# Column marks of a sparse four-layer graph network: summed by halves on GpSimd instead of a maximum on VectorE

## The chip, the cores and the metric

The kernel runs on one core of a Trainium2 chip. The metric is the device time of one execution in microseconds (us): before the change the median of three runs is 1175.17 us (1168.04 to 1184.51). The profiled execution has a span of 1172.0 us from its first to its last instruction. The engines of the core are called as the profile calls them: PE (TensorE matmul), PEld (its weight load), DVE (VectorE), ACT (ScalarE), POOL (GpSimd), SP (SyncE, which here only issues transfers).

## What is computed

Four layers of a graph network run over x (4096 rows of 128 features) and an adjacency matrix adj (4096 x 4096). Each layer is x = x + layer(relu(layernorm(x)), adj). Layers 0 and 1 multiply adj with the features (once and twice), layer 2 is an attention over the marked pairs, and layer 3 sums GELU messages over them:

```python
neigh = adj @ x                                               # layer 0
T_next = 2.0 * (L_tilde @ T_curr) - T_prev                    # layer 1, after T_curr = L_tilde @ x
Tau = adj_matrix.T * jnp.exp(jnp.maximum(0.2 * C, C))         # layer 2
messages = jax.nn.gelu(s[:, None, :] + d[None, :, :] + msg_b, approximate=False)
aggregated = jnp.einsum('ijd,ij->id', messages, adj)          # layer 3
```

Most of adj is zero. An entry (i, j) off the diagonal is non-zero with a probability that falls with both i and j, so the first rows and columns are dense and the rest is nearly empty. The kernel finds the non-zero entries once, while it runs layer 0, and from then on works with lists.

## The kernel before

The matrix is taken in 32 blocks of 128 rows (NB), in 16 stripes of 256 rows (ROWS) and in 16 stripes of 256 columns (COLS). For each stripe the blocks that are dense enough are read whole ("near"). The other rows or columns that have an entry in the stripe form a list, cut into chunks of 128, and each chunk is fetched by an indirect gather that POOL issues (line 551).

**Finding the entries.** For each block b of 128 rows, two halves of 1 MB are read by `read_adj` (line 766 issues on SP's queue) into three buffers. `mark` (line 776, ACT) turns each half into one byte per element, 0x38 for a non-zero, in one of four mask tiles (128 x 4096 bytes, or 1024 words of four elements). Then `scan` works on DVE, in this order: line 787 clears the diagonal in the block's own 32 words; line 791 takes, for each of the 16 column stripes, the maximum of its 64 words, and writes it to column b of `col_raw` (128 x 16 x 32); line 796 ORs the word's number into the mask (tile `words`, 128 x 1024); line 798 multiplies by "mask is non-empty", so that words without an entry become zero; and line 805 takes the eight largest words of each segment (MAX8), which are the candidates for the entry lists.

**Row lists.** `row_flags` counts the marks of a row stripe with matmuls on PE (line 704), and `pairs` (lines 641 to 681, DVE, with ACT line 630 and PE lines 645, 646 and 664 between) makes the stripe's list, `fetch_row` and `seg_row`. Layer 0 then gathers, on POOL, for each chunk of the list one tile of adjT (`rseg`, eight buffers) and one of features (`g`, fourteen buffers), PE multiplies them (line 1163), and SP stores `rseg` to a table for the later layers (line 730). Where 512 columns of the result are complete, ACT copies them (line 1172), PE multiplies with the weights (line 604), and DVE adds them to x (line 1000) and normalises.

**Column lists.** They need the marks of all 32 blocks: `all_marked` is set after the last block's line 791. `col_flags` (line 717) then compares `col_raw` of one stripe with EMPTY and runs the same `pairs`; `fetch_columns` gathers the adj chunks (`cseg`), which layer 2 reads.

**The order of the work.** Every step is a Python generator that says which engine it wants and for how long. A planner runs these against a model of the engines while the program is written, and the resulting order is fixed on every engine: each executes its instructions strictly in the order in which the planner recorded them. A step that asks for a tile waits for a free slot (`Slots`), and `give_back` returns the slot when a `Count` of its readers has come to zero. Where the planner sees PE idle it adds filler matmuls (line 617) that keep its clock up. POOL's order holds constants, 12 additions of a bias to x (lines 987 and 1008), and 724 gathers: per layer those for layer 0 (`rseg`, `g` from h_tab), the column chunks (`cseg`), layer 1 (`g` from h_tab and u_tab), the values of single entries (`e_val`), layer 2 (`g` from a_tab) and layer 3 (`m`, `tau` and `e` from d_tab).

Of the kernel before, what the change touches and what calls it, by code (L numbers as in the profile page):

```python
# [12 lines left out]
F32 = mybir.dt.float32  # L13
# [5 lines left out]
I32 = mybir.dt.int32  # L19
AF = mybir.ActivationFunctionType  # L20
ALU = mybir.AluOpType
AX = mybir.AxisListType
# [5 lines left out]
P = 128  # L28
NB = N // P
# [10 lines left out]
EMPTY = struct.unpack("<f", b"\x30" * 4)[0]  # L40
WORDS = N // 4
# [76 lines left out]
RS, CS = 256, 256  # L118
# [3 lines left out]
COLS = [Stripe(i, CS, C_EXTRA) for i in range(N // CS)]  # L122
# [235 lines left out]
def on_dve(n):  # L358
    return "DVE", 0.16 + 1.05e-3 * n
# [19 lines left out]
def sparse_stack(tc, x, adj, adjT, diag, w_self, w_neigh, b0, w1, b1, w2, att_src, att_dst,  # L379
# [7 lines left out]
    nc = tc.nc  # L387
    plan = Plan()
    EARLY = 7
    with ExitStack() as ctx:  # L390
# [4 lines left out]
        def tiles(pool, name, n, shape, dtype=F32):  # L395
            return Slots([pool.tile(list(shape), dtype, name=f"{name}{i}", tag=f"{name}{i}") for i in range(n)])

        def kept(name, shape, dtype=F32):
            return keep.tile(list(shape), dtype, name=name, tag=name)
# [114 lines left out]
        col_raw = kept("col_raw", (P, len(COLS), NB))  # L514
# [198 lines left out]
        def col_flags(s):  # L713
            yield all_marked
            lane = yield lanes
            yield on_dve(NB)
            nc.vector.tensor_scalar(lane["f"], col_raw[:, s.index, :], EMPTY, None, op0=ALU.is_gt)
            yield from pairs(s, lane, fetch_col, seg_col, CS, col_list[s.index])

        row_list = [Event() for _ in ROWS]  # L720
        col_list = [Event() for _ in COLS]
        r_done = [Count(s.cap) for s in ROWS]
        c_done = [Count(s.cap) for s in COLS]
        all_marked = Event()

        def store(ready, t, slots, left, dst, done, size):

# [7 lines left out]
        def give_back(left, slots, t):  # L735
            yield left
            plan.release(slots, t, left.time)
# [23 lines left out]
        def read_adj():  # L761
            for b in range(NB):
                for h in range(2):
                    a = yield raws
                    yield SP
                    nc.sync.dma_start(a, adj[b * P:(b + 1) * P, h * HALF:(h + 1) * HALF])
                    raw_of[b, h] = a
                    raw_here[b][h].set(plan.transfer(P * HALF * 4))

        def mark():  # L770
            for b in range(NB):
                mask_of[b] = mask = yield masks
                for h in range(2):
                    yield raw_here[b][h]
                    yield on_act(HALF + 200, "sigmoid")
                    nc.scalar.activation(mask[:, h * HALF:(h + 1) * HALF], raw_of[b, h], AF.Sigmoid, scale=1e38,  # L776
                                         accum_out=marks[:, 2 * b + h:2 * b + h + 1], saturate=False)
                    plan.release(raws, raw_of[b, h])
                marked[b].set(plan.finish)

        def scan():
            for b in range(NB):
                yield marked[b]
                mask = mask_of[b]
                yield on_dve(32)
                own = mask.bitcast(I32)[:, b * P // 4:(b + 1) * P // 4]
                nc.vector.tensor_tensor(own, own, off_diag.bitcast(I32), op=ALU.bitwise_and)
                bare[b].set(plan.finish)
                plan.start(give_back(mask_left[b], masks, mask), 0)
                yield on_dve(WORDS)  # L790
                nc.vector.tensor_reduce(col_raw[:, :, b], mask.bitcast(F32).rearrange("p (s w) -> p s w", w=CS // 4),
                                        axis=AX.X, op=ALU.max)
                if b == NB - 1:
                    all_marked.set(plan.finish)
                yield on_dve(WORDS)
                nc.vector.tensor_tensor(words, mask.bitcast(I32), spread, op=ALU.bitwise_or)
                yield on_dve(WORDS + 250)
                nc.vector.scalar_tensor_tensor(words.bitcast(F32), mask.bitcast(F32), EMPTY, words.bitcast(F32),
                                               op0=ALU.is_gt, op1=ALU.mult)
                mask_left[b].set(plan.finish)  # L800
                for u in UNITS:
                    if u.block == b:
                        yield "DVE", 0.15 * len(u.segments) + (u.cuts[-1] - u.cuts[0]) / 960
                        for k, (lo, hi) in enumerate(u.segments):
                            nc.vector.max(cand_of[u.number][:, 8 * k:8 * k + 8], words.bitcast(F32)[:, lo:hi])
                        picked[u.number].set(plan.finish)

        picked = [Event() for _ in UNITS]
        valued = [Count(u.cap) for u in UNITS]
# [154 lines left out]
        def read_x():  # L964
            for g in range(NC):
                yield SP
                nc.sync.dma_start(xN[:, g * GB:(g + 1) * GB, :], x_rows[:, g * GB:(g + 1) * GB, :])
                x_here[g].set(plan.transfer(P * BANK * 4))
                if g == 1:
                    for tab in (h_tabs[0], h_tabs[1], u_tab):  # L970
                        nc.sync.dma_start(tab[N:N + 1, :], zero[:, :D])
                    nc.sync.dma_start(a_tab[N:N + 1, :], zero)

        def begin(g):
            yield x_here[g]
            yield x_here[g + 1]
            blocks = slice(g * GB, (g + 2) * GB)
            yield from norm(blocks, hA[:, blocks, :])
            for k in range(2):
                h_done[g + k].set(plan.finish)  # L980
            yield SP
            nc.sync.dma_start(rows_in(h_tabs[0])[:, blocks, :], hA[:, blocks, :])
            landed = plan.transfer(2 * P * BANK * 4)
            for k in range(2):
                h0_table.set(landed)
            yield "POOL", 2.5
            nc.gpsimd.tensor_add(xN[:, blocks, :], xN[:, blocks, :], by_block(b0_sb, 2 * GB))
            for k in range(2):
                blocks = slice((g + k) * GB, (g + k + 1) * GB)
                yield from to_features(blocks, hA[:, blocks, :])  # L990
# [492 lines left out]
        def weights():  # L1483

            yield "DVE", 0.5
            nc.vector.tensor_sub(w02, w1_sb[:, 0, :], w1_sb[:, 2, :])
            nc.vector.tensor_scalar_mul(w22, w1_sb[:, 2, :], 2.0)
            p = yield banks
            yield on_pe(P)
            nc.tensor.transpose(p[:, :P], w2_sb[:, :D], ident)  # L1490
            yield on_act(P)
            nc.scalar.copy(w2T, p[:, :P])
            yield on_pe(2)
            nc.tensor.matmul(p[:, P:P + 2], w2T, att_sb, start=True, stop=True)
            yield "DVE", 0.5
            nc.vector.tensor_copy(w2_sb[:, D:], p[:, P:P + 2])
            nc.vector.tensor_copy(dst_w, w2_sb[:, D + 1:D + 2].to_broadcast([P, P]))
            plan.release(banks, p)
# [68 lines left out]
        with tc.tile_pool(name="scan", bufs=1) as scanning:  # L1567
            rsegs = tiles(scanning, "rseg", 2048 // RS, (P, RS))
            masks = tiles(scanning, "mask", 4, (P, N), F8)
            raws = tiles(scanning, "raw", 1, (P, HALF))  # L1570
            raws = Slots([dst[:, :HALF], dst[:, HALF:]] + raws.items)
            words = scanning.tile([P, WORDS], I32, name="words", tag="words")
            plan.filler = fill
            plan.start(read_x(), -9)
            plan.start(read_adj(), -8)
            for g in range(0, NC, 2):
                plan.start(begin(g), g * 1e-2 - 8.5)
            plan.start(mark(), -8.6)
            plan.start(scan(), -4)
            plan.start(weights(), 3)  # L1580
            for s in ROWS:
                if s.cap:
                    plan.start(row_flags(s), -9)
            for part in (loads, gathers, products):
                plan.start(part(), 0)
            for s in COLS:
                if s.cap:
                    plan.start(col_flags(s), s.index * 1e-2 - 1.5)
            plan.start(fetch_columns(), 4)
            plan.run(lambda: layers[0].through.time is not None and all(p.time is not None for p in picked)  # L1590
                     and len(rsegs.free) == len(rsegs.items))
# [5 lines left out]
        for i in range(2):  # L1597
            def lane_tile(name, width, dtype=F32):
                return second.tile([P, width], dtype, name=f"{name}_{i}", tag=f"{name}_{i}")
            lane = {k: lane_tile(k, -(-most // 2) + 2 * GB) for k in ("et", "ev", "epop", "ecum", "evf")}  # L1600
# [3 lines left out]
            n = max(sum(u.cap for u in g.units) for g in GROUPS)  # L1604
# [403 lines left out]
```

## Time and profile before

| What | us |
|---|---|
| median of three runs | 1175.17 |
| profiled execution, span | 1172.0 |
| first gather on POOL (`rseg`) | at 87.24 |
| last of 32 maxima (line 791) begins | at 325.53 |
| first column gather (`cseg`) | at 348.03 |
| last gather's issue ends | at 1141.35 |
| 32 maxima, line 791, busy in all | 39.1 |
| 32 ORs, line 796 | 39.5 |
| 32 products, line 798 | 39.1 |
| POOL busy, share of the span | 771.8, 66% |

The page gives, for each engine, busy time and share, then the span in 40 slices whose digits are tenths of busy time, then the costliest groups of instructions: line, engine, operation, output and inputs, count, busy time, mean duration of one in ns, and the idle time of the engine just before them with what ended it. The timeline lists instructions in order with their start and duration; idle time ahead of one stands in brackets with what released it. Idle time of an engine that is not the bottleneck costs nothing.

### The profile page before, as it was taken

To read this page: it belongs to the slowest core of one execution; us is meant where nothing else is said; L and a number is where in the kernel's file an instruction comes from. 1 tells how busy PE (TensorE), PEld (TensorE's weight loads), DVE (VectorE), ACT (ScalarE), POOL (GpSimd) and SP (SyncE) were. 2 spreads that over 40 slices of the span, in tenths; PEclk is the share of its full clock that TensorE was granted. 3 is DMA by queue.
4 is the path that set the end of the run, shared out by engine and by line. 5 is a ranking of instruction groups with operands and counts; after the bars stand their busy time and mean duration, and the time that the engine had idled before them with its cause. 6 is when DMAs were issued, how large, how long until landed. Compare 5 with 4: busy or idle time off the path is not lost. (4 is left out here: it accounts for less than half of the span.)

```text
span 1172.0 us, 19272 instructions
## 1 busy us (share of the span) xinstructions
PE 965.2 (82%) x5782; PEld 669.7 (57%) x5782; DVE 887.9 (76%) x3443; ACT 577.5 (49%) x1228; POOL 771.8 (66%) x831
## 2 busy tenths in 40 slices
PE   5888887878888888788888879899999976678783
PEld 2555665545555665576676654455555555566562
DVE  5799988877878886576888866665666585577895
ACT  3985556654622212232434457576767652234553
POOL 5127746545437677777777778777777777777770
PEclk9979989888789999998989989898999878889997
DMA  7999999999846978889865653443445222222321
GB/s 221 348 349 394 349 407 359 352 309 334 294 127 174 301 217 275 245 272 315 247 204 175 184 150 97 127 129 102 131 131 154 71 69 67 54 68 68 77 74 33
DMA packets 175417, 236.04 MB, mean 201 GB/s; under 512 B 22452, under 2 KB 155336, under 8 KB 167112
## 3 DMA queue, kind: packets, MB, share of 16 engines
q1 hardware_dynamic: 148904, 186.45, 46.9%
q0 software_dynamic: 26400, 48.27, 16.7%
q8 instruction: 48, 0.79, 0.3%
q14 instruction: 65, 0.53, 0.1%
HBM read 203.41 MB, written 31.23 MB: 200 GB/s over the span
## 5 line engine op out<-in xcount | busy, mean ns | idle before, releaser
L551 POOL DMA_INDIRECT e_val<-in_adj,e_at x158 | 163.0, 1032 | 48.0 <-issue 40.1
L551 POOL DMA_INDIRECT g<-h_tab,fetch_row x136 | 134.6, 990 | 41.1 <-issue 27.9
L551 POOL DMA_INDIRECT rseg<-in_adjT,seg_row x68 | 68.8, 1012 | 90.3 <-issue 42.3
L1146 PE MATMUL acc<-big,hA 128*128 128x256 f32 x448 | 122.0, 415 | 2.0 <-DMA big<-in_adjT 2.0
L617 PEld LDWEIGHTS <-nothing 128*128 128x128 f16 x732 | 74.9, 105 | 82.0 <-issue 20.7
L617 PE MATMUL pick<-nothing 128*128 128x512 f16 x430 | 114.2, 413 | 0.0
L551 POOL DMA_INDIRECT cseg<-in_adj,seg_col x74 | 70.9, 958 | 43.6 <-issue 17.3
L1146 PEld LDWEIGHTS acc<-big,hA 128*128 128x128 f32 x448 | 89.4, 210 | 14.5 <-DMA big<-in_adjT 2.6
L776 ACT ACTIVATE mask<-dst 128x2048 fp8e4<-128x2048 f32 x43 | 81.8, 1904 | 26.8 <-DMA dst<-in_adj 26.7
L551 POOL DMA_INDIRECT m<-d_tab,e_col x79 | 76.8, 972 | 24.1 <-issue 13.4
L551 POOL DMA_INDIRECT g<-a_tab,fetch_col x74 | 75.7, 1023 | 22.5 <-issue 12.5
L1163 PE MATMUL acc<-big,g 128*128 128x256 f32 x272 | 77.4, 417 | 9.7 <-DMA big<-r_tab 6.5
L1243 DVE TENSOR_TENSOR tau<-e,big 128x512 f32<-128x512 f32 (+3 forms) x61 | 54.5, 893 | 38.2 <-ACT e L1239 34.0
L551 POOL DMA_INDIRECT tau<-d_tab,e_col x67 | 66.2, 988 | 21.2 <-issue 11.3
L617 PE MATMUL bank<-nothing 128*128 128x512 f16 x302 | 79.8, 401 | 0.0
L551 POOL DMA_INDIRECT g<-u_tab,fetch_row x68 | 64.5, 949 | 20.7 <-issue 8.8
L577 ACT ACTIVATE junk<-xN,stat 128x128 f32<-128x128 f32 x128 | 51.3, 401 | 49.0 <-DVE stat L573 38.5
L1146 PE MATMUL acc<-big,hB 128*128 128x256 f32 x224 | 60.9, 411 | 11.3 <-DMA big<-in_adjT 11.3
L1163 PE MATMUL acc<-rseg,g 128*128 128x256 f32 x136 | 53.4, 501 | 16.8 <-DMA g<-h_tab,fetch_row 16.7
L898 DVE SCALAR_TENSOR_TENSOR ehit<-ehit,pos,pick 128x32 f32<-128x32 f32 (+7 forms) x158 | 38.7, 285 | 36.2 <-ACT ehit L895 35.9
L1163 PEld LDWEIGHTS acc<-big,g 128*128 128x128 f32 x272 | 52.6, 207 | 21.4 <-issue 7.5
L895 ACT COPY ehit<-pick 128x192 f32<-128x192 f32 (+7 forms) x74 | 20.4, 287 | 89.3 <-PE pick L892 78.1
(322 smaller groups left out, 2553.1 us busy)
## 6 DMA issues: line engine op xcount, KB each, us to landing
dst<-in_adj SPq DMA_DIRECT2D x43, 1024.0 KB
big<-in_adjT SPq DMA_DIRECT2D x45, 512.0 KB
raw<-in_adj SPq DMA_DIRECT2D x21, 1024.0 KB
big<-in_adjT SPq DMA_DIRECT2D x66, 256.0 KB
big<-r_tab SPq DMA_DIRECT2D x30, 512.0 KB
c_tab<-cseg SPq DMA_DIRECT2D x74, 128.0 KB
r_tab<-rseg SPq DMA_DIRECT2D x68, 128.0 KB
big<-c_tab SPq DMA_DIRECT2D x15, 512.0 KB
```

What stands on the lines that cost most here:

```text
L551: nc.gpsimd.indirect_dma_start(out=dst, out_offset=None, in_=table[:, :], in_offset=bass.IndirectOffsetOnAxis(ap=index, axis=0))
L577: nc.scalar.activation(junk, src[:, k, :], AF.Square, bias=st[:, 0, k:k + 1], accum_out=st[:, 1, k:k + 1])
L617: nc.tensor.matmul(idle[2][idle[1]], nothing[:, :P], nothing, start=True, stop=True)
L776: nc.scalar.activation(mask[:, h * HALF:(h + 1) * HALF], raw_of[b, h], AF.Sigmoid, scale=1e38, accum_out=marks[:, 2 * b + h:2 * b + h + 1] ...
L895: nc.scalar.copy(hit, pv[:, :, :W])
L898: nc.vector.scalar_tensor_tensor(hit[:, q, :], hit[:, q, :], pos0[:, k + q:k + q + 1], pv[:, q, W:2 * W], op0=ALU.is_le, op1=ALU.mult, acc ...
L1146: nc.tensor.matmul(acc, self.near[:, b, :D], as_rows(t)[:, k, :], start=count == 0, stop=count == every - 1)
L1163: nc.tensor.matmul(acc, row[:, :D], r, start=count == 0, stop=count == every - 1)
L1243: nc.vector.tensor_mul(tau[:, :n, :], e[:, :n, :], a[:, :n, :])
```

## The change

The maximum on line 791 goes. In its place POOL sums the masked words: a new step `marks_of_columns` adds the upper half of each stripe's 64 words to the lower half, and so on down to one word, in six additions per block (512, 256, 128, 64, 32 and 16 elements per partition). The words that line 798 has cleaned are its input, so it starts after that line and not before line 796. `words` becomes two tiles taken in turn, given back when both the additions and the MAX8 of the block are planned as done. `halved` (128 x 16 x 32) holds the partial sums. `all_marked` now counts 32 blocks' sums, and `col_flags` compares with 0.0.

```diff
-            nc.vector.tensor_scalar(lane["f"], col_raw[:, s.index, :], EMPTY, None, op0=ALU.is_gt)
+            nc.vector.tensor_scalar(lane["f"], col_raw[:, s.index, :], 0.0, None, op0=ALU.is_gt)
...
-        all_marked = Event()
+        all_marked = Count(NB)
...
+        def marks_of_columns(b, words, left):
+
+            sums = words.bitcast(F32).rearrange("p (s w) -> p s w", w=CS // 4)
+            n = CS // 8
+            yield "POOL", 3.1
+            while n:
+                into = halved[:, :, :n] if n > 1 else col_raw[:, :, b:b + 1]
+                nc.gpsimd.tensor_add(into, sums[:, :, :n], sums[:, :, n:2 * n])
+                sums, n = halved, n // 2
+            left.set(plan.finish)
+            all_marked.set(plan.finish)
+
...
-                yield on_dve(WORDS)
-                nc.vector.tensor_reduce(col_raw[:, :, b], mask.bitcast(F32).rearrange("p (s w) -> p s w", w=CS // 4),
-                                        axis=AX.X, op=ALU.max)
-                if b == NB - 1:
-                    all_marked.set(plan.finish)
+                words = yield words_of
...
                 mask_left[b].set(plan.finish)
+                left = Count(2)
+                plan.start(marks_of_columns(b, words, left), -4)
+                plan.start(give_back(left, words_of, words), 0)
...
                         picked[u.number].set(plan.finish)
+                left.set(plan.finish)
...
-            words = scanning.tile([P, WORDS], I32, name="words", tag="words")
+            words_of = tiles(scanning, "words", 2, (P, WORDS), I32)
+            halved = scanning.tile([P, len(COLS), CS // 8], F32, name="halved", tag="halved")
```

Because the planner places every step anew, the fixed orders change too. On POOL the 192 additions stand among layer 0's gathers: those of five blocks ahead of the first gather, and from there those of one block after every three to seven gathers. All 68 pairs of layer 0's gathers now stand ahead of the first column gather (64 pairs before), so 588 gathers follow from there instead of 596. The fillers on PE are 748 instead of 732.

## The prediction

> **What bounds the kernel now.** I read the page's busy shares and slices first, then three stretches of the span, then POOL's timeline, then single rows.
>
> ```profile
> PE 965.2 (82%) x5782; PEld 669.7 (57%) x5782; DVE 887.9 (76%) x3443; ACT 577.5 (49%) x1228; POOL 771.8 (66%) x831
> ...
> POOL 5127746545437677777777778777777777777770
> ...
> DMA  7999999999846978889865653443445222222321
> ```
>
> POOL's digit is 7 from slice 15 to the end, never 9. The three stretches (columns: PE, PEld, DVE, ACT, POOL busy, then granted PE clock, DMA share, GB/s) say why:
>
> ```profile
> 39.14:87.24 48.10, 38.34 (x276) 25.74 (x274) 42.02 (x170) 43.15 (x88) 10.26 (x4) 0.83 0.99 352
> 87.24:348.03 260.79, 217.97 (x1706) 146.61 (x1704) 222.76 (x701) 143.97 (x221) 139.74 (x136) 0.86 0.92 329
> 348.03:1141.35 793.32, 670.48 (x3609) 474.77 (x3608) 579.10 (x2440) 361.41 (x843) 601.80 (x610) 0.93 0.54 154
> ```
>
> In the last stretch POOL is busy 601.80 of 793.32 us in 610 instructions, so 191.5/610 = 0.31 us lie ahead of each; the timeline shows 0.30 us of "issue" ahead of nearly every gather. POOL is thus full from 348.03 to 1141.35: 596 gathers every 1.25 to 1.35 us. The last 31 us are layer 3's tail. So the end is set by when POOL has done all its work, and the stretch before 348.03 matters by how much of that work is left then.
>
> In that first part POOL waits (timeline; start, duration, idle before):
>
> ```profile
> 226.97 1.19 POOL L551 DMA_INDIRECT rseg<-in_adjT,seg_row  x1 [6.33 <-PE acc L1163]
> ...
> 243.34 0.94 POOL L551 DMA_INDIRECT rseg<-in_adjT,seg_row  x1 [6.25 <-issue]
> ...
> 257.45 1.27 POOL L1008 TENSOR_TENSOR xN<-xN,b_sb 128x512 f32<-128x512 f32 x1 [3.46 <-issue]
> 265.04 1.19 POOL L551 DMA_INDIRECT rseg<-in_adjT,seg_row  x1 [6.31 <-PE acc L1163]
> ...
> 348.03 0.96 POOL L551 DMA_INDIRECT cseg<-in_adj,seg_col  x1 [14.61 <-DVE pf L641]
> ```
>
> The pattern repeats every 37.6 us (L1008 at 219.37, 257.45, 295.01, 332.16), one period for four blocks: POOL waits for `rseg` buffers, for a row list from DVE, for the bias step. Adding its waits over 0.5 us after 87.24 gives 71.2 us, and 14.6 us ahead of the first column gather: 85.8 us of room in all. DVE is busy 222.76 of 260.79 there (85%) and the DMA share is 0.92, so three resources are nearly full together.
>
> **What is removed.** 32 maxima on DVE, 39.1 us:
>
> ```profile
> L791 DVE TENSOR_REDUCE col_raw<-mask 128x16 f32<-128x1024 f32 x32 | 39.1, 1221 | 2.1 <-ACT mask L776 0.4
> L1008 POOL TENSOR_TENSOR xN<-xN,b_sb 128x512 f32<-128x512 f32 x8 | 10.5, 1310 | 10.4 <-issue 6.9 <-ACT hB L585 3.4
> L987 POOL TENSOR_TENSOR xN<-xN,b_sb 128x1024 f32<-128x1024 f32 x4 | 10.3, 2565 | 47.4 <-ACT hA L585 45.6 <-DVE pair_total L649 1.8
> ```
>
> **What is added.** 192 POOL additions. The two rows above are the same operation at two sizes. Undisturbed they take 1.264 and 2.350 us (the shortest of each), so one element costs 1.086/512 = 2.12 ns and an instruction 0.18 us. The six sizes 512, 256, 128, 64, 32, 16 give 1.26 + 0.72 + 0.45 + 0.31 + 0.25 + 0.21 = 3.21 us a block. The trace has no addition that waits for the one before on POOL; the nearest gaps are 0.02 us (gather to L1008) and 0.14 us (L1008 to the next gather). I take 0.08 and keep both ends. Five blocks' sums stand ahead of the first gather, in POOL's idle time (37.8 us between 39.14 and 87.24): free. The other 27 blocks cost 27 x 3.21 = 86.6 us, plus 162 gaps of 0.08 = 13 us (3 to 23).
>
> **The two engines block each other.** While L1008 runs, DVE instructions with two inputs stand still:
>
> ```profile
> 257.48 1.26 DVE L651 SCALAR_TENSOR_TENSOR pst<-pst 128x1 f32<-128x1 f32 x1
> ...
> 273.85 0.16 DVE L651 SCALAR_TENSOR_TENSOR pst<-pst 128x1 f32<-128x1 f32 x1
> ```
>
> The first ends when the addition begun at 257.45 ends, 1.10 us late. The other instances, each against its usual duration: L787 at 43.31 (+1.14), L642 at 68.99 (+1.80), 137.05 (+0.72) and 159.35 (+1.71), L651 at 72.76 (+2.16), 218.84 (+1.67) and 295.09 (+1.05), L796 at 195.02 (+0.54), L717 at 332.77 (+0.53): 12.4 us lost on DVE to the eleven additions up to 332.16, which took 19.5 us, or 0.64 us for each of POOL's. Those additions met DVE anywhere. The new ones begin behind line 798, where DVE enters MAX8 (1.4 us, one input, and unhindered when POOL added at 39.14). So DVE loses between nothing and 0.64 x 32 x 3.21 = 66 us for its 39.1 saved; from the rows I take half, 33 us, which leaves DVE about where it was (-6 us).
>
> The Trainium skill, page "SBUF — State Buffer", section "SBUF: two separate sides", calls the port pair of the two engines an exclusive lock: a DVE instruction with two SBUF inputs and a GpSimd instruction that reads SBUF never overlap, and the later one waits out the earlier. By it the cost could not be read as a share of overlap: lines 787, 796 and 798 (2.6 us) and the sums (3.2 us) would simply follow one another, and DVE's saving of 1.22 us a block would be gone with the first addition met. The rows agree for the instructions named.
>
> The other way round, POOL waits for DVE: the twelve L987 and L1008 exceed their shortest by 0.83 + 0.37 = 1.2 us, 0.10 us each. For 162 additions that is 16 us; the bounds are nothing, and one whole L796 (1.22 us) a block, 33 us.
>
> **What of POOL's room stays a wait.** The sums can use a wait only if they are queued at it and their words are ready. A later POOL finds `rseg` buffers free, and the 14.6 us is filled by ten gathers that the new order puts behind the last sums. But behind each block's sums stand three to seven gathers: these land later, so does PE line 1163, then lines 1172, 604 and 1000, and behind line 1000 DVE's next mask. I take a fifth of the room as staying, 17 us (0 to half, 43).
>
> **Other edits.** The second `words` tile lets DVE write block b+1 while POOL still reads b; DVE's line 796 now waits for the first addition of block b-2. Queued behind it are the row lists, and POOL waits for those. It costs nothing while POOL lags under two blocks (19 us); otherwise it is the rival below. The threshold changes no time. Eight gathers and two bias steps moved ahead of the first column gather delay it by 12.6 us and shorten what follows by the same. Sixteen fillers sit in PE's planned gaps: nothing, or 16 x 0.41 = 7 us if not hidden. SP's order keeps its transfers.
>
> **The sum.** 86.6 + 13 + 16 + 17 - 85.8 = +47 us on the span, so 1172 + 47 = 1219, and 3 us around it (median against span): **1222 us**. Ends: 86.6 + 3 - 85.8 - 6 (five maxima gone before 87 us) = -2 gives 1173; 86.6 + 23 + 33 + 43 + 7 - 85.8 = +107 gives 1282.
>
> **Rivals.** *POOL's waits swallow everything*: the sums fall into the 85.8 us and only the gaps and a few blocked microseconds remain, +0 to +15, 1175 to 1190. For it: the room is nearly the right size, about 16 us in each period of 37.6 for 12.8 us of sums. Against it: the waits come two or three at a time, the sums every 9.4 us. Chance 0.18. *Faster*: DVE sets the pace of the scan (85% busy, its row list is what ends one POOL wait a period), and 27 x 1.22 = 33 us come off the first column gather. It decides if DVE's loss to the blocking stays under about 10 us and the sums fit. Bytes allow it: 112 MB pass before 348.03 (247, 352 and 329 GB/s up to 39.14, 87.24 and 348.03), at the 371 GB/s of 50 to 225 us they need 303 us. 1175 - 33 = 1142, with partial forms up to 1160. Chance 0.10. *The ring closes*: POOL waits for `rseg` buffers with sums behind, DVE waits at line 796 for words, no row list comes. One such stall of 6.3 us in each of 6.5 periods on top of +47 gives +88, 1263. Chance 0.12. The rest, 0.60, is the forecast, itself between 1190 and 1250.
>
> **Chances.** 2% is 23.5 us, about what a measurement of this kernel can tell. Faster (under 1151.7): 0.09. Within: the swallowing rival and the low part of the forecast, 0.21. Slower: 0.70. Range 1168 to 1262: it leaves the fast rival and the worst of the ring outside.
>
> **What would show it.** First column gather near 348 + 12.6 + 47 = 405 to 410; POOL without long waits between 90 and that; six additions a block of 3.2 to 3.7 us; L642, L651, L796 longer on average; the stretch from the first column gather to the last about 12 us shorter than 793. The forecast is wrong if the first column gather comes before about 370, or if POOL still has 60 us of long waits.

## The result and the profile after

The changed kernel takes **1214.92 us** (median of four runs, 1213.06 to 1219.25); the kernel before took 1173.94 us beside it (1168.04 to 1184.51). The ratio is 1.033, with a 95% interval of 1.029 to 1.037 (the quotient of the two medians, 1.035, lies in it): slower, 41 us by the medians. Here and below a median is taken over all runs of a kernel, and a ratio over its undisturbed runs alone. The profiled execution has a span of 1211.2 us, 39.2 more than before. The forecast was 1222.

The page's busy shares, and GpSimd's and the DMA's slices, of the changed kernel:

```profile
PE 978.4 (81%) x5798; PEld 675.5 (56%) x5798; DVE 883.3 (73%) x3411; ACT 576.6 (48%) x1228; POOL 890.9 (74%) x1023
...
POOL 5568888888877677777777777777777776777770
...
DMA  7999899899866977888976562344445422222321
```

POOL's digits are now 8 in slices 4 to 11, where they were 4 to 7, and from there on mostly 7, as before. VectorE gave up 39.1 us of maxima and is only 4.6 us less busy (887.9 before). The DMA's digits fall to 8 in slices where they were 9.

Three stretches of the changed kernel, from the first gather to the first column gather, from there to the end of the last gather, and the tail (columns as in the prediction):

```profile
80.67:386.89 306.22, 239.37 (x1764) 158.69 (x1763) 225.62 (x694) 145.04 (x226) 248.18 (x305) 0.80 0.85 285
386.89:1182.27 795.38, 672.04 (x3623) 475.65 (x3624) 579.12 (x2431) 360.79 (x842) 599.43 (x605) 0.94 0.54 154
1182.27:1211.20 28.93, 10.40 (x75) 8.27 (x73) 16.93 (x56) 9.16 (x27) 0.00 (x0) 0.78 0.09 24
```

The prediction closed the middle stretch of the kernel before at 1141.35, where three gathers were still to come. To the end of the last one it reads:

```profile
348.03:1145.49 797.46, 674.62 (x3644) 478.76 (x3643) 583.24 (x2454) 361.41 (x843) 605.03 (x613) 0.93 0.54 154
```

So the 39.2 us are made of: first gather 6.6 us earlier (80.67 against 87.24), first stretch 45.4 us longer (306.22 against 260.79), middle stretch 2.1 us shorter, tail 2.4 us longer. All of the loss lies ahead of the first column gather.

The counts of gathers on record ahead of the result (724, and 596 or 588 from the first column gather on) leave out the twelve of tile `e` in layer 3. The traces have 736, and 608 before and 600 after. The difference of eight, on which the forecast rests, stands.

POOL's groups in that first stretch of the changed kernel, by line and form (count; busy, mean ns; idle ahead of them and what ended it):

```profile
L551 POOL DMA_INDIRECT rseg<-in_adjT,seg_row x68 | 71.6, 1052 | 29.2 <-issue 17.8 <-PE acc L1175 4.6 <-DVE mask L799 1.9
L551 POOL DMA_INDIRECT g<-h_tab,fetch_row x68 | 69.4, 1020 | 18.8 <-issue 14.0 <-DVE sel L632 0.6 <-DVE hit L667 0.6
L788 POOL TENSOR_TENSOR halved<-words 128x512 f32<-128x512 f32 x27 | 35.4, 1310 | 1.0 <-DVE pf L709 0.5
L788 POOL TENSOR_TENSOR halved<-halved 128x256 f32<-128x256 f32 x27 | 21.6, 799 | 2.1
L788 POOL TENSOR_TENSOR halved<-halved 128x128 f32<-128x128 f32 x27 | 16.6, 614 | 2.1
L788 POOL TENSOR_TENSOR halved<-halved 128x64 f32<-128x64 f32 x27 | 11.3, 419 | 2.1
L1020 POOL TENSOR_TENSOR xN<-xN,b_sb 128x512 f32<-128x512 f32 x7 | 8.9, 1269 | 0.1
L788 POOL TENSOR_TENSOR halved<-halved 128x32 f32<-128x32 f32 x27 | 6.9, 255 | 2.1
L788 POOL TENSOR_TENSOR col_raw<-halved 128x16 f32<-128x16 f32 x27 | 6.8, 253 | 2.1
```

These rows and those below are for that stretch alone. The six rows of line 788 make 98.6 us, and 10.5 us of idle time stand between dependent additions (five rows of 2.1, so 0.08 us each). The bias step (line 1008 before, 1020 now) runs seven times on both sides. The same rows of the kernel before:

```profile
L551 POOL DMA_INDIRECT g<-h_tab,fetch_row x64 | 65.5, 1023 | 19.2 <-issue 15.7 <-DMA rseg<-in_adjT,seg_row 2.7 <-DMA big<-in_adjT 0.3
L551 POOL DMA_INDIRECT rseg<-in_adjT,seg_row x64 | 65.0, 1016 | 89.0 <-issue 41.1 <-PE acc L1163 28.3 <-DVE pf L641 12.2
```

The idle time ahead of the `rseg` gathers is where the room was: 89.0 us before, 29.2 after, most of which is the 0.3 us that lies ahead of any gather. As a ledger of POOL's time from the first gather to the first column gather (waits are all those over 0.5 us; "other idle" is the rest):

| us | before | after |
|---|---|---|
| row gathers (128, 136) | 130.5 | 141.0 |
| 7 bias steps | 9.2 | 8.9 |
| sums of 27 blocks | 0 | 98.6 |
| gaps between additions | 0 | 10.5 |
| waits | 85.8 | 12.2 |
| other idle | 35.3 | 35.0 |
| stretch | 260.8 | 306.2 |

POOL took on 109.1 us and 10.5 us of gathers, and 73.6 us of waits went. Such a ledger adds up by construction; what it tells is that the waits are nearly used up.

PE is slower in that stretch too: its granted clock is 0.80 against 0.86, and it is busy for 239.37 us against 217.97. But the waits for PE ahead of the `rseg` gathers fell from 28.3 to 4.6 us, and all of POOL's waits over 0.5 us are 12.2, so a later PE can account for no more than that. The DMA share fell from 0.92 to 0.85, so the transfers aren't what is short either.

The timeline of the changed kernel's POOL shows sums that wait for nothing (start, duration, idle ahead):

```profile
249.77 0.95 POOL L551 DMA_INDIRECT rseg<-in_adjT,seg_row  x1 [0.31 <-issue]
250.74 1.28 POOL L788 TENSOR_TENSOR halved<-words 128x512 f32<-128x512 f32 x1
252.09 1.98 POOL L788 TENSOR_TENSOR halved<-halved 128x256 f32<-128x256 f32 x4
254.15 0.22 POOL L788 TENSOR_TENSOR col_raw<-halved 128x16 f32<-128x16 f32 x1
254.51 0.95 POOL L551 DMA_INDIRECT g<-h_tab,fetch_row  x1
...
386.89 0.94 POOL L551 DMA_INDIRECT cseg<-in_adj,seg_col  x1 [0.30 <-DVE sel L632]
```

All 27 first additions together have 1.0 us of idle time ahead of them: the words were there when POOL came to them. The first column gather, which stood behind 14.61 us of idle time before, now follows the gather ahead of it at once: POOL itself is what is late. While the sum begun at 250.74 runs, VectorE stands still:

```profile
250.14 1.96 DVE L642 TENSOR_TENSOR_SCAN pcum<-ones,pf 128x32 f32<-128x32 f32 x1
```

It usually takes 0.28 us; here it ends at 252.10, as the addition begun at 250.74 ends (252.02). Its recorded start lies 0.60 us ahead of the addition's, so the two starts alone don't tell which of the two is held up; its length does.

### The profile page after: what moved, and what is told of

Its sections match the earlier page's. It is cut to its first block, busy times and chain, and to the rows that moved or that the text cites. A ratio compares the mean times of both kernels' runs of the same rounds, so it can differ in the third digit from the quotient of the medians.

```text
span 1211.2 us, 19481 instructions
## 1 busy us (share of the span) xinstructions
PE 978.4 (81%) x5798; PEld 675.5 (56%) x5798; DVE 883.3 (73%) x3411; ACT 576.6 (48%) x1228; POOL 890.9 (74%) x1023
## 4 chain that ended last, share of the span: by engine, by line
DVE 28%; DMA 23%; PE 17%; POOL 14%; issue 10%; ACT 6%; SPq 1%; DVEq 0%; POOLq 0%; ACTq 0%
POOL e_val L551 5%; DMA g<-h_tab,fetch_row 4%; DMA g<-a_tab,fetch_col 4%; PE acc L1158 3%; DMA cseg<-in_adj,seg_col 3%; POOL halved L788 3%; POOL g L551 3%; DMA m<-d_tab,e_col 2%; PE acc L1175 2%; DMA tau<-d_tab,e_col 2%; DMA dst<-in_adj 2%; PE bank L604 2%; DMA c_tab<-cseg 1%; PE acc L1274 1%; PE acc L1272 1%
## 5 line engine op out<-in xcount | busy, mean ns | idle before, releaser
L1158 PE MATMUL acc<-big,hA 128*128 128x256 f32 x448 | 127.7, 428 | 1.6 <-DMA big<-in_adjT 1.6
L617 PEld LDWEIGHTS <-nothing 128*128 128x128 f16 x748 | 78.4, 107 | 86.4 <-issue 23.3
L551 POOL DMA_INDIRECT g<-a_tab,fetch_col x74 | 78.2, 1056 | 22.6 <-issue 12.8
L551 POOL DMA_INDIRECT rseg<-in_adjT,seg_row x68 | 71.6, 1052 | 29.2 <-issue 17.8
L617 PE MATMUL bank<-nothing 128*128 128x512 f16 x327 | 85.1, 396 | 0.0
L788 POOL TENSOR_TENSOR halved<-halved 128x256 f32<-128x256 f32 (+3 forms) x128 | 66.1, 516 | 10.0
L788 POOL TENSOR_TENSOR halved<-words 128x512 f32<-128x512 f32 x32 | 41.7, 1303 | 33.8 <-DVE words L806 28.9
L907 ACT COPY ehit<-pick 128x192 f32<-128x192 f32 (+9 forms) x74 | 20.2, 286 | 94.7 <-PE pick L904 69.9
```

Source lines behind the costliest of these rows:

```text
L551: nc.gpsimd.indirect_dma_start(out=dst, out_offset=None, in_=table[:, :], in_offset=bass.IndirectOffsetOnAxis(ap=index, axis=0))
L617: nc.tensor.matmul(idle[2][idle[1]], nothing[:, :P], nothing, start=True, stop=True)
L788: nc.gpsimd.tensor_add(into, sums[:, :, :n], sums[:, :, n:2 * n])
L907: nc.scalar.copy(hit, pv[:, :, :W])
L1158: nc.tensor.matmul(acc, self.near[:, b, :D], as_rows(t)[:, k, :], start=count == 0, stop=count == every - 1)
```

## The experiments

Three theories were held against each other. **A**: the sums cost GpSimd's own time, as far as it exceeds the waits that GpSimd had ahead of the first column gather. **B**: they cost because GpSimd's reading and VectorE's two-input instructions hold each other up. **C**: the new fixed order and the second tile of words carry the loss, whatever the sums do.

The runs fell on two kinds of chip. Those whose labels are ghost2, memset2 and both2 ran where the kernel before takes 1173.56 us (seven runs). The other nine ran on chips on which the kernel before itself takes 1507 to 1511 us; they are told last.

### The sums left out (ghost2)

All 192 additions go, and no maximum comes back: the column marks are not computed. `col_raw` is preset: for each stripe as many whole blocks, evenly spaced, as its list has chunks of 128 are marked. So as many column gathers run as before, of other rows. The order on all engines is that of the changed kernel.

```diff
+        nc.gpsimd.memset(col_raw, 0.0)
+        for s in COLS:
+            others = [b for b in range(NB) if b not in s.near]
+            for k in range(s.cap):
+                b = others[k * len(others) // s.cap]
+                nc.gpsimd.memset(col_raw[:, s.index, b:b + 1], 1.0)
...
-            while n:
-                into = halved[:, :, :n] if n > 1 else col_raw[:, :, b:b + 1]
-                nc.gpsimd.tensor_add(into, sums[:, :, :n], sums[:, :, n:2 * n])
-                sums, n = halved, n // 2
```

> The kernel of ghost once more (the changed kernel in its own fixed order, the 192 additions left out, no maximum on VectorE, column marks set beforehand), beside the kernel before at its usual time near 1174 us. Theory A (GpSimd's own time for the sums sets the delay): 1140 to 1172 us, ratio 0.97 to 1.00. Theory B (mutual blocking): the same. Theory C (the new fixed order costs): 1200 to 1216 us, ratio 1.02 to 1.035.

Measured: 1156.12 us (1153.56 to 1160.14), ratio to before 0.987 (0.984 to 0.991). Its first two stretches:

```profile
78.13:329.58 251.45, 218.45 (x1763) 147.26 (x1761) 194.66 (x694) 147.37 (x227) 151.58 (x143) 0.88 0.96 350
329.58:1123.41 793.83, 667.47 (x3622) 471.81 (x3623) 577.26 (x2432) 360.48 (x842) 598.32 (x605) 0.94 0.52 154
```

A and B expect the same here; the run tests C. C falls: the same order and the second tile without the sums are 17 us faster than before, so the sums themselves cost 59 us (1214.92 - 1156.12; 54 by the ratios). The 17 us are what VectorE's relief, the new order and the second tile are worth together; no run has the relief alone. POOL's waits are back, 61.4 us of them:

```profile
267.70 1.41 POOL L557 DMA_INDIRECT rseg<-in_adjT,seg_row  x1 [7.08 <-issue]
...
301.99 1.41 POOL L557 DMA_INDIRECT rseg<-in_adjT,seg_row  x1 [6.08 <-issue]
```

### GpSimd's time without its reading (memset2)

As ghost2, but each block's six additions become seven memsets of `halved`, which hold GpSimd about as long and read nothing. The marks are again not computed.

```diff
+            flat = halved.rearrange("p s w -> p (s w)")
+            for size in 6 * [512] + [256]:
+                nc.gpsimd.memset(flat[:, :size], 0.0)
```

> The kernel of memset once more (seven memsets a block of about the same total time on GpSimd in the place of the six additions, column marks set beforehand). Theory A: GpSimd full in the same way, within 12 us of the changed kernel, 1203 to 1218 us. Theory B: no two engines read at once, so within 12 us of ghost2.

Measured: 1202.83 us (1202.28 to 1207.28), ratio 1.027 (1.024 to 1.031). First stretch, and POOL's memsets in it:

```profile
80.50:378.65 298.15, 235.59 (x1763) 155.08 (x1761) 207.73 (x694) 147.09 (x227) 244.41 (x332) 0.81 0.86 295
```

```profile
L794 POOL MEMSET halved<- 128x512 f32 x162 | 86.4, 533 | 7.8
L794 POOL MEMSET halved<- 128x256 f32 x27 | 8.5, 316 | 1.5
```

Of the 59 us, 47 (1202.83 - 1156.12) come back with memsets alone: A, though the run ends just under A's range and 12.1 us below the changed kernel, where 12 was the limit. The ledger: the memsets take 94.9 us and 9.3 us of gaps, POOL's waits fall from 61.4 to 5.8 us, and 104.2 - 55.6 = 48.6 us are left; the first column gather comes 49.1 us later than in ghost2.

What remains beyond the memsets is 12 us by the medians, some 7 by the ratios, whose intervals overlap a little; the additions' own 3.7 us more than the memsets are in it. That isn't yet all that B can claim. The memsets were made as long as the sums took, and some 12 us of the sums' 98.6 were waits for VectorE (estimated below), which these 47 us count as GpSimd's time. With them B is at most about 24 of the 59 us, two fifths. So it is shown that GpSimd's time sets the price, and left open how much of that time is blocking.

### The maxima back on VectorE as well (both2)

The changed kernel in its order, with the 32 maxima back on VectorE ahead of line 804. They fill `col_raw`; the sums still run and their last addition writes a tile that nothing reads.

```diff
-            nc.vector.tensor_scalar(lane["f"], col_raw[:, s.index, :], 0.0, None, op0=ALU.is_gt)
+            nc.vector.tensor_scalar(lane["f"], col_raw[:, s.index, :], EMPTY, None, op0=ALU.is_gt)
...
-                into = halved[:, :, :n] if n > 1 else col_raw[:, :, b:b + 1]
+                into = halved[:, :, :n] if n > 1 else unused
...
+                nc.vector.tensor_reduce(col_raw[:, :, b], mask.bitcast(F32).rearrange("p (s w) -> p s w", w=CS // 4),
+                                        axis=AX.X, op=ALU.max)
```

> The kernel of both once more (the changed kernel in its own order, the maxima back on VectorE and used, the additions kept on GpSimd and unused). Theory A: 1215 to 1228 us, since VectorE is not what is late. Theory B: VectorE carries 39 us more on the path, 1238 to 1255 us.

Measured: 1218.99 us (1216.02 to 1221.12), ratio 1.039 (1.036 to 1.043). First stretch:

```profile
82.45:394.22 311.77, 239.33 (x1765) 156.97 (x1763) 257.31 (x721) 144.48 (x226) 248.79 (x306) 0.81 0.82 279
```

VectorE carries 31.7 us more in this stretch than in the changed kernel (257.31 against 225.62) and 38.4 in all, and the time rises by 4 us (7 by the ratios; the first column gather comes 7.3 us later). Once POOL is full, VectorE's work is nearly free, so taking 39 us from it gains little as long as the sums are there.

### On the other chips

There the granted clock is 0.80 to 0.83 (0.89 to 0.92 on the usual chip), the engines often stand with nothing that the trace shows releasing them, and POOL is little more than half busy to the end. What makes these chips slower isn't known. The page's busy shares and POOL's slices of ghost there:

```profile
PE 1044.1 (70%) x5798; PEld 715.1 (48%) x5798; DVE 845.6 (57%) x3411; ACT 574.8 (39%) x1228; POOL 769.0 (52%) x906
...
POOL 5153544444555556445655752665654717566630
```

The kernels are those above, and three more. In oneadd, the first addition of a block (512 elements) is all that is left of the sums, with `col_raw` preset as in ghost2. In early, POOL sums blocks 0 to 4 alone, ahead of its first gather, and the rest keep the maximum on VectorE; in alternate, POOL sums these five and every odd block behind them. Both of the last have two tiles of words and an order planned anew.

```diff
+            nc.gpsimd.tensor_add(halved, sums[:, :, :n], sums[:, :, n:])
```

```diff
+                on_pool = b < 5
+                if not on_pool:
+                    yield on_dve(WORDS)
+                    nc.vector.tensor_reduce(col_raw[:, :, b],
+                                            mask.bitcast(F32).rearrange("p (s w) -> p s w", w=CS // 4),
+                                            axis=AX.X, op=ALU.max)
+                    all_marked.set(plan.finish)
...
-                left = Count(2)
-                plan.start(marks_of_columns(b, words, left), -4)
+                left = Count(1 + on_pool)
+                if on_pool:
+                    plan.start(marks_of_columns(b, words, left), -4)
```

```diff
-                on_pool = b < 5
+                on_pool = b < 5 or b % 2 == 1
```

For ghost, the sums left out:

> The changed kernel in its own fixed order, with the 192 additions on GpSimd left out and no maximum on VectorE; the column marks are set beforehand to as many rows per stripe as its list holds, so the lists have their usual length but not the right rows. Theory A (GpSimd's own time for the sums sets the delay): the 41 us of the change come back and VectorE's 39 us of relief show, 1140 to 1172 us, first column gather before 348 us. Theory B (the two engines block each other, VectorE is late with its lists): the same, as nothing blocks. Theory C (the new fixed order costs, not the sums): stays near the changed kernel, 1200 to 1216 us.

For memset, seven memsets a block in their place:

> As ghost, but in the place of each block's six additions GpSimd runs seven memsets of about the same total time (estimate 4.1 us a block with gaps, as six additions take 3.62 us and 0.08 us each between), which read nothing; column marks set beforehand as in ghost. Theory A: GpSimd is full in the same way, 1200 to 1218 us, within 12 us of the changed kernel. Theory B: without two engines reading there is no blocking, so within 12 us of ghost.

For oneadd:

> As ghost, but with the first of each block's six additions (128x512, 1.30 us); column marks set beforehand. Theory A: 27 blocks x 1.38 us = 37 us fall into GpSimd's 85.8 us of waits, so 0 to 15 us above ghost. Theory B: the cost goes with the time in which GpSimd reads, 1.30 of 3.62 us, so ghost plus about 0.36 of the difference between ghost and the changed kernel (some 15 to 25 us).

For both, the maxima back as well:

> The changed kernel in its own order, with the 32 maxima back on VectorE (39.1 us) and used for the lists, and the six additions of each block kept on GpSimd, their result unused. Theory A: VectorE is not what is late, 1215 to 1228 us. Theory B: VectorE is the late engine and carries 39 us more, 1238 to 1255 us.

For oneadd2, the kernel of oneadd on another chip:

> Only the first of the six additions of a block is left (512 elements per partition, 1.30 us in the trace of the changed kernel); the other 160 are left out, and col_raw is preset as in ghost2. Theory A (GpSimd's own time counts, once its room is used up): the sums now take 27 x (1.30 + 0.08) = 37 us, which fits into the 64 us in which ghost2's GpSimd waits ahead of the first column gather; 0 to 15 us above ghost2, 1156 to 1171, first column gather 330 to 345. Theory B (what costs is that GpSimd reads the masked words while VectorE wants two inputs): the first addition is 42 of 116 us of reading, 0.36 x 59 = 21 us above ghost2, 1177, first column gather near 350.

For early:

> GpSimd sums the marks of blocks 0 to 4 alone, which it does ahead of its first gather, where it is idle; the other 27 blocks have their maximum on VectorE again; two tiles of words as in the change; the order is planned anew. Theory A: the five blocks cost GpSimd nothing, five maxima (6.1 us) leave VectorE ahead of the first gather, which came 6.6 us earlier in the changed kernel: first gather near 81, time 0 to 7 us below the kernel before, 1167 to 1174. Theory B (the blocking alone costs 12 us per 27 blocks, and VectorE loses what it saves): 1172 to 1178, first gather at 85 to 87. Theory C (the second tile of words and the new order carry the loss): above 1185.

For alternate:

> GpSimd sums the marks of blocks 0 to 4 and of every odd block after them, 19 of 32; the other 13 keep the maximum on VectorE. Theory A (a room of 86 us ahead of the first column gather, only what goes beyond it costs): 14 blocks x 4.1 us (3.62 and six gaps of 0.08) = 57 us behind the first gather, inside the room; the time stays within -8 to +8 us of the kernel before, 1166 to 1182, and GpSimd keeps 20 to 35 us of waits over 0.5 us ahead of the first column gather. Theory B (each block's sums cost their share whatever room there is): 14/27 of 41 us = +21, 1195.

For early2, the kernel of early on a third chip:

> The kernel of run early once more, for a chip on which the kernel before takes its usual 1174 us. GpSimd sums the marks of blocks 0 to 4 alone, ahead of its first gather; the other 27 blocks have their maximum on VectorE. Theory A (only GpSimd time beyond its waits costs): the five blocks are free and five maxima, 6.1 us, leave VectorE ahead of the first gather: first gather at 80 to 83, first column gather 340 to 348, time 1167 to 1174. Theory B (reading blocks VectorE for as much as the maxima took): 1172 to 1178, first gather at 85 to 87.

For alternate2, the kernel of alternate there:

> The kernel of run alternate once more, for a chip on which the kernel before takes its usual 1174 us. GpSimd sums blocks 0 to 4 and every odd block after them, 19 of 32. Theory A: 14 blocks x 4.1 us (3.62 and six gaps of 0.08) = 57 us behind the first gather, inside the room of 86 us: -8 to +8 us, 1166 to 1182, first column gather 342 to 358, and GpSimd keeps 20 to 35 us of waits over 0.5 us ahead of it. Theory B (each block's sums cost their share whatever room there is): 14/27 of 41 us = +21, 1195, first column gather near 369.

| run | us | before, us | ratio (95%) |
|---|---|---|---|
| ghost | 1491.33 | 1511.48 | 0.989 (0.981 to 0.996) |
| memset | 1484.99 | 1511.48 | 0.982 (0.974 to 0.990) |
| oneadd | 1485.53 | 1511.48 | 0.982 (0.975 to 0.989) |
| both | 1504.38 | 1511.48 | 0.996 (0.991 to 1.000) |
| oneadd2 | 1475.5 | 1507.51 | 0.976 (0.968 to 0.984) |
| early | 1507.87 | 1507.51 | 0.998 (0.994 to 1.002) |
| alternate | 1521.92 | 1507.51 | 1.009 (1.004 to 1.015) |
| early2 | 1515.89 | 1509.46 | 1.001 (0.996 to 1.007) |
| alternate2 | 1526.99 | 1509.46 | 1.013 (1.007 to 1.019) |

The expectations in microseconds, made for the usual chip, can't be held against these times. One thing can be read: the memsets, 112 us of POOL's time, cost nothing over ghost here, where they cost 47 us above. From the first gather to the first column gather, ghost and then memset (columns as before):

```profile
80.66:391.76 311.10, 239.03 (x1771) 155.26 (x1769) 195.23 (x694) 147.16 (x227) 147.15 (x144) 0.81 0.82 283
78.67:379.86 301.19, 230.87 (x1772) 152.72 (x1770) 207.77 (x694) 147.21 (x227) 244.44 (x332) 0.84 0.85 292
```

POOL's waits over 0.5 us in this stretch are 129.5 us in ghost, more than the 104.1 that the memsets take there with their gaps, and 9.3 in memset; the first column gather comes no later. On the usual chip ghost2 had 61.4 us of waits for 104.2 us of memsets, and 49 us were lost. A price that hangs on POOL's free time is what A says. It is support, not proof: here POOL has free time behind that stretch too, and the ratios of the two runs overlap.

The dose was not settled: oneadd is no slower than ghost, but no theory could show a loss where even the memsets' time is free. The hope that early would be faster than the kernel before was not met where it ran, since it is level with it; on the usual chip it, oneadd and alternate did not run. Alternate's 1% is not explained either: it asks less of POOL and of VectorE than both, which is 0.4% below before, and its order is its own. That stays open.

## Why the prediction was right

The forecast's mechanism held: POOL's time ahead of the first column gather, its room of 85.8 us used up, the rest late. Its terms, against the ledger:

- **The sums.** 86.6 us and 16 of waiting for VectorE made 102.6; measured 98.6, so the waiting took 12.0 (3.65 us a block against 3.21). The price was right: the shortest additions of the six sizes take 1.251, 0.726, 0.449, 0.316, 0.237 and 0.218 us, 86.3 us for 27 blocks. That what lies above the shortest is waiting for VectorE is inferred from the durations. The gaps were put at 13 and are 10.5, at the 0.08 us that was taken.
- **Room that stays a wait.** 17 forecast, 12.2 measured. So 98.6 + 10.5 + 12.2 - 85.8 = 35.5, where the sum had 47.
- **VectorE ahead of the first gather.** The sum took nothing for the five maxima gone there, and 6 us in its low end only; the first gather comes 6.6 us earlier, at 80.67. The size is that of the low end's term, but the reason is mostly another: in both2 the maxima are back, and its first gather still comes at 82.45, 4.8 us earlier than before. By these traces, one of each kernel, the maxima account for some 2 of the 6.6 us, and the rest came with the new order and the second tile.
- **The eight gathers moved ahead.** Forecast to cost 12.6 us there and to give it back behind. Two things were wrong in this step. The two bias steps did not move (seven ahead of the first column gather in both), so the cost was 10.5. And only 2.1 us came back: POOL's waits behind the first column gather rose from 9.5 to 16.5 us, in the `cseg` row those for the stores of `c_tab` from 5.8 to 10.0, and one ahead of a `tau` gather from 1.1 to 3.8. The runs ghost2, memset2 and both2, which share the order, have 793.1 to 795.0 us in this stretch and 14.4 to 16.1 us of such waits, whatever their sums: it goes with the order, not with the sums. That column gathers no longer have row gathers between them, which gave the stores time, is read from the timeline and wasn't tried.

The first column gather was forecast at 405 to 410 and came at 386.89. The errors add up to the 20 us: 4 for the waiting, 2.5 for gaps, 5 for room, 6.6 for the first gather, 2 for the moved gathers. Nearly 13 us of that was made up for by errors the other way: 10.5 us of gain behind it that failed and 2.4 us more of tail. So the time ended 7 us under the forecast, near for a reason that was partly luck.

**VectorE.** It was to lose 33 us to the blocking and end 6 us less busy. In ghost2 it is busy for 845.3 us, in the changed kernel, with the same instructions, for 883.3: 38.0 us lost, and 4.6 us less than before. The three lines named as signs, in the changed kernel:

```profile
L804 DVE TENSOR_TENSOR words<-mask,spread 128x1024 int32<-128x1024 int32 x32 | 44.4, 1388 | 5.3 <-ACT mask L776 2.2
...
L642 DVE TENSOR_TENSOR_SCAN pcum<-ones,pf 128x32 f32<-128x32 f32 x30 | 12.2, 405 | 1.1
...
L651 DVE SCALAR_TENSOR_TENSOR pst<-pst 128x1 f32<-128x1 f32 x30 | 10.3, 344 | 1.0
```

and in ghost2:

```profile
L806 DVE TENSOR_TENSOR words<-mask,spread 128x1024 int32<-128x1024 int32 x32 | 39.2, 1224 | 6.6 <-ACT mask L782 5.2
...
L648 DVE TENSOR_TENSOR_SCAN pcum<-ones,pf 128x32 f32<-128x32 f32 x30 | 8.4, 280 | 1.1
L657 DVE SCALAR_TENSOR_TENSOR pst<-pst 128x1 f32<-128x1 f32 x30 | 4.8, 160 | 1.0
```

Line 804 takes 164 ns more on average, line 642 125 and line 651 184. That is 14.5 of the 38 us; the rest lies on other lines.

**The rivals.** *POOL's waits swallow everything* fell because the waits were used to 86% but were 23 us too few: 109.1 us of sums and gaps for 85.8. *Faster* needed VectorE's loss under 10 us, and sums that fit; the loss was 38 and they did not fit. *The ring closes* did not happen: only 5.3 us of idle time stand ahead of all 32 of line 804, and POOL's longest wait in the first stretch is 2.40 us. Nor did the change fail to do its work: no maximum is left in the trace, and 192 additions run.

## What to carry to other kernels

Before work is moved to an engine that looks two thirds busy, add up its waits stage by stage, and count the fixed gap ahead of each instruction as full: here 34% idle was 86 us of real room, and 109 us went into it. What the relieved engine gains is measured by leaving the work out altogether (17 us here, the new order with it), and if that is less than the price on the other engine, the move can't win. A forecast that gives back later what it delays now should look at what wait stands behind, since it need not come back.

## What the hardware showed

VectorE's loss has two forms, and memset2 tells them apart. Its VectorE rows, from the timeline (start, duration):

```profile
142.97 1.16 DVE L657 SCALAR_TENSOR_TENSOR pst<-pst 128x1 f32<-128x1 f32 x1
...
94.39 0.55 DVE L686 TENSOR_SCALAR prow<-prow 128x6 f32<-128x6 f32 x1
94.97 0.55 DVE L687 TENSOR_SCALAR seg_row<-prow 128x6 uint32<-128x6 f32 x1
```

and what its POOL did at these times:

```profile
142.83 1.27 POOL L1025 TENSOR_TENSOR xN<-xN,b_sb 128x512 f32<-128x512 f32 x1
...
92.01 3.85 POOL L794 MEMSET halved<- 128x512 f32 x7
```

The two-input instruction (0.16 us usually) waits for the addition, which reads, and ends with it. Memsets, which only write, leave it alone: its three instances that lie wholly under a row of memsets (at 85.09, 204.94 and 248.41) take 0.16 us. One-input TENSOR_SCALAR instructions (0.17 us usually) take 0.55 there, about one memset of 0.53. So a GpSimd instruction that reads nothing isn't free for VectorE: it lost 15.3 us to the memsets (860.6 against 845.3). The Trainium skill, page "SBUF — State Buffer", section "Who interferes with whom", names both cases: two inputs contend only with a GpSimd instruction that reads, while a VectorE instruction in a two-port mode, which TENSOR_SCALAR can enter, contends with GpSimd without that condition. The two rows agree with it. Line 717, which the prediction lists among the two-input instructions held up, is a TENSOR_SCALAR with one input (0.68 us at 332.77 against 0.17 usually), so by the page it would be of the second case.

In the changed kernel VectorE lost 38.0 us, 22.7 more than in memset2, and the two kernels lie at most some 12 us apart. That so much loss on an engine that is 73% busy costs so little fits both2, where 38.4 us more of VectorE's work cost 4: VectorE was not what was late.
